# Routing pieces and shared-expert groups in another order, in a two-layer model kernel

## The chip, the cores and the metric

The kernel runs on one core of a Trainium2 chip. Its time is the device time of one execution in microseconds (us), here the median of four runs. A profile of one further execution gives each engine's instructions with their start and duration: TensorE (PE, with its weight loads as PEld), VectorE (DVE), ScalarE (ACT), GpSimd (POOL), and SyncE (SP), which issues most DMA transfers. All data are float32.

## The reference, cut to what matters

Two layers over T = 4096 tokens of D = 128 features. Each layer adds to its input an attention and a mixture of experts, both computed from the same normalised input.

```
xn = layernorm(x)
x  = x + window_attention(layernorm(xn)) + ffn0(xn)        # layer 0
xn = layernorm(x)
x  = x + gated_attention(layernorm(xn)) + ffn1(xn)         # layer 1

ffn0(xn):
    probs   = softmax(xn @ router_w + router_b)            # 8 experts
    weights = probs at the two largest, 0 elsewhere
    shared  = gelu(xn @ sw1 + sb1) @ sw2 + sb2
    experts = gelu(xn @ rw1[e] + rb1[e]) @ rw2[e] + rb2[e] # H = 256
    return shared + sum over e of weights[e] * experts[e]
```

The window attention has 16 batches of 256 tokens, 8 heads of 64, rotated queries and keys, and a softmax over 256 keys in two windows. ffn1 has 32 experts with hidden size 64, eight of them for each token.

## The kernel before, in words

The tokens lie in 8 groups of 512 (NG = 8), each four chunks of 128 (NC = 4).

**Attention of layer 0.** The order of PE, DVE, ACT and POOL is written out by hand: a loop over s from -2 to 64, in which a step s in 0 to 63 is one pair of heads and one batch, eight steps for a group g (r = s % 8). A step issues, in this order:

- `turned0(s)`: PE transposes the probabilities p (L413);
- `exponentials(s + 1)`: ACT, with a sum beside each (L395), then `evicted(s)`: ACT copies the transposed tiles to pT (L420);
- what steps before had put off: copies of the values v on ACT (L339), and in even steps the rotations of q and k (L359 to L361, on DVE and POOL);
- a piece or two of the routing, and pieces of `prepare`;
- `divided(s + 1)`: DVE's reciprocal (L401) and four products (L404);
- `scores(s + 2)`: PE (L379), then DVE's masked maximum (L384) and its negation (L388);
- `attended(s - 1)`: PE (L430), ACT (L435); and `project` of the group before at r = 2: PE (L441), ACT (L443).

The routing of a group is a generator of five pieces, `routed` with `route0` inside: (1) two normalisations, DVE with POOL's powers; (2) transposes and a copy to xnT; (3) the router's matmuls; (4) logits less their maximum on DVE, and their exponential pr_all on ACT (L220); (5) on DVE the sum of pr_all (L223), reciprocal, product, and the rank of each expert by comparisons (L196 to L205). The call of a step is

```
step(routing, 2 * g + 2 + r // 4, (1, 1, 1, 2)[r % 4])
```

so that a group's five pieces are spread over four steps, and pieces 4 and 5 come together in a step with r % 4 == 3.

`places0` (L231 to L293) turns the ranks of all tokens into row places: running counts over 32 chunks (five doublings), three matmuls that sum over partitions (pos_ps and cnt_ps, L253 the last), and from these where each token's two rows stand (slot_at), their weights (slot_w), and which expert each of 39 tiles of 256 rows has (tile_off). Before, it runs whole at s = 26. `scatter0(n)` writes chunk n's rows to x_rows in HBM, two indirect DMAs on POOL (L298) for each step from 27 to 58.

**Shared expert and expert tiles.** Behind the attention SyncE issues twelve loads of layer-1 weights (uvu to sd, L76, 1.34 MB together). `shared0(g)` transposes the weights of group g (L179; wT copied by DVE, L181), multiplies them with rb2 (L549), computes two hidden halves hs (L552, gelu at L554), adds them up with sw2 in y (L555), and adds y to yTs[g] on DVE (L556). Then 39 tiles go through four stages, each some tiles behind the other (0, 4, 5, 6): `fetched` (SyncE loads we, L572, and xt, L574, six buffers of each), `turned` (PE transposes, L585, DVE copy, L587), `hidden` (PE L594, ACT gelu L597), `down` (PE L604, DVE copy, SyncE writes y_rows, L610). Every xt waits for all scatters. The weights eg, eu and ed of layer 1, 1 MB each, are loaded last on the same queue.

**Layer 1.** `finish0(g)` gathers a token's two rows from y_rows, eight indirect DMAs on POOL for a group (L636), into yg, a single buffer; PE transposes yTs[g], DVE adds it to x (L645), adds the gathered rows with their weights (L648), and normalises; xn1T follows on PE. Routing, gated attention and 17 pairs of experts for each group stand behind it.

Of the kernel before, what the change touches and what calls it, by code (L numbers as in the profile page):

```python
# [23 lines left out]
NG = T // G  # L24
# [23 lines left out]
def two_layers(ctx: ExitStack, tc: tile.TileContext, a: dict, out: bass.AP):  # L48
# [182 lines left out]
    def places0(wk):  # L231

        nch = NG * NC
        fl = lambda t: t.rearrange("p n e -> p (n e)")
        top, sel = (wk.tile([P, nch, E0], F32, tag=f"m{i}", name=f"m{i}", bufs=1) for i in range(2))
        nc.vector.tensor_scalar(fl(sel), fl(rk_all), 2.0, None, ALU.is_lt)
        nc.vector.tensor_scalar(fl(top), fl(rk_all), 0.0, None, ALU.is_equal)
        nc.vector.tensor_tensor(fl(w0_all), fl(sel), fl(pr_all), ALU.mult)

        acc = sel  # L240
        for i in range(5):
            k = 1 << i
            nxt = wk.tile([P, nch, E0], F32, tag=f"cum{i % 2}", name=f"cum{i}", bufs=1)
            nc.vector.tensor_copy(nxt[:, :k, :], acc[:, :k, :])
            nc.vector.tensor_tensor(nxt[:, k:, :], acc[:, k:, :], acc[:, : nch - k, :], ALU.add)
            acc = nxt
        ex = wk.tile([P, nch, E0], F32, tag="ex", name="ex", bufs=1)
        nc.vector.tensor_tensor(ex, acc, sel, ALU.subtract)
        pos_ps = mm_tile("pos_ps")[:, : nch * E0]
        nc.tensor.matmul(pos_ps, upper, fl(sel), start=True, stop=False)  # L250
        nc.tensor.matmul(pos_ps, ones, fl(ex), start=False, stop=True)
        cnt = mm_tile("cnt_ps")[:, :E0]
        nc.tensor.matmul(cnt, ones, acc[:, nch - 1, :], start=True, stop=True)  # L253
        ns = T // RT
        full = wk.tile([P, E0, ns], F32, tag="full", name="full", bufs=1)
        nc.vector.tensor_tensor(
            full, cnt.unsqueeze(2).to_broadcast([P, E0, ns]), steps.unsqueeze(1).to_broadcast([P, E0, ns]), ALU.is_gt
        )
        used = wk.tile([P, E0], F32, tag="used", name="used", bufs=1)
        nc.vector.tensor_reduce(used, full, AX.X, ALU.add)  # L260
        low = wk.tile([P, E0, E0], F32, tag="low", name="low", bufs=1)
        nc.vector.tensor_tensor(
            low, used.unsqueeze(1).to_broadcast([P, E0, E0]), tie0.rearrange("p (i j) -> p i j", j=E0), ALU.mult
        )
        begin = wk.tile([P, E0], F32, tag="begin", name="begin", bufs=1)
        nc.vector.tensor_reduce(begin, low, AX.X, ALU.add)
        row0 = wk.tile([P, E0], F32, tag="row0", name="row0", bufs=1)
        nc.vector.tensor_scalar(row0, begin, float(RT), None, ALU.mult)
        pos = wk.tile([P, nch, E0], F32, tag="pos", name="pos", bufs=1)
        nc.vector.tensor_tensor(  # L270
            pos, pos_ps.rearrange("p (n e) -> p n e", e=E0), row0.unsqueeze(1).to_broadcast([P, nch, E0]), ALU.add
        )
        nc.vector.tensor_tensor(fl(sel), fl(sel), fl(top), ALU.subtract)
        for s, m in enumerate((top, sel)):
            at = wk.tile([P, nch, E0], F32, tag="at", name=f"at{s}", bufs=1)
            nc.vector.tensor_tensor(at, m, pos, ALU.mult)
            atr = wk.tile([P, nch], F32, tag="atr", name=f"atr{s}", bufs=1)
            nc.vector.tensor_reduce(atr, at, AX.X, ALU.add)
            nc.vector.tensor_copy(slot_at[:, s, :], atr)
        for s, m in enumerate((top, sel)):  # L280
            nc.vector.tensor_tensor(m, m, pr_all, ALU.mult)
            nc.vector.tensor_reduce(slot_w[:, s, :], m, AX.X, ALU.add)

        le = wk.tile([P, NT0, E0], F32, tag="le", name="le", bufs=1)
        nc.vector.tensor_tensor(
            le, begin.unsqueeze(1).to_broadcast([P, NT0, E0]), tiles.unsqueeze(2).to_broadcast([P, NT0, E0]), ALU.is_le
        )
        ex_t = wk.tile([P, NT0], F32, tag="ex_t", name="ex_t", bufs=1)
        nc.vector.tensor_reduce(ex_t, le, AX.X, ALU.add)
        nc.vector.tensor_scalar(ex_t, ex_t, -1.0, None, ALU.add)  # L290
        off = wk.tile([P, NT0], F32, tag="off", name="off", bufs=1)
        nc.vector.tensor_scalar(off, ex_t, float(P), None, ALU.mult)
        nc.vector.tensor_copy(tile_off, off)  # L293

    def scatter0(n):

# [12 lines left out]
    with first as pa:  # L309
        wk = pa.enter_context(tc.tile_pool(name="wkA", bufs=2))  # L310
# [138 lines left out]
        with tc.manual_schedule(engines={order.PE, order.DVE, order.Activation, order.Pool}):  # L449
            routing = {g: routed(g) for g in range(NG)}  # L450
            preparing = {g: prepare(g) for g in range(NG)}

            def step(gens, g, n=1):
                if 0 <= g < NG:
                    for _ in range(n):
                        next(gens[g], None)

            step(routing, 0)
            step(preparing, 0, 2)
            rotated(0)  # L460
            for f in turning:
                f()
            turning.clear()
            step(routing, 0, 2)
            step(routing, 1)
            step(preparing, 1)
            for c in range(NC):
                values(0, c)
            for f in later:
                f()  # L470
            later.clear()
            step(routing, 0, 2)
            step(routing, 1)
            rotated(1)
            for s in range(-2, NS + 1):
                g, r = divmod(s, 8)
                if 0 <= s < NS:
                    tps = turned0(s, sc.pop(s)[0])
                if 0 <= s + 1 < NS:
                    sms[s + 1] = exponentials(s + 1, *sc[s + 1])  # L480
                if 0 <= s < NS:
                    pTs[s] = evicted(s, tps)
                for f in later:
                    f()
                later.clear()
                for f in turning:
                    f()
                turning.clear()

                if s < 0:  # L490
                    step(routing, 1, 2)
                else:
                    step(routing, 2 * g + 2 + r // 4, (1, 1, 1, 2)[r % 4])
                if r == 0:
                    step(preparing, g + 1)
                if s >= 0 and r == 6:
                    step(preparing, g + 2)
                if 0 <= s + 1 < NS:
                    divided(s + 1, sc[s + 1][0], sms.pop(s + 1))
                if s + 2 < NS:  # L500
                    sc[s + 2] = scores(s + 2)
                if s >= 1:
                    attended(s - 1, pTs.pop(s - 1))

                if s % 2 and 2 <= (s + 5) // 2 < NS // 2:
                    rotated((s + 5) // 2)
                if s < 0:
                    continue
                if r == 2 and g:
                    project(g - 1)  # L510
                if r in (4, 6) and g + 1 < NG:
                    values(g + 1, r - 4)
                    values(g + 1, r - 3)
                if s == 10:
                    zero = w_a.tile([P, 2 * D], F32, tag="zero", name="zero")
                    nc.gpsimd.memset(zero, 0.0)
                    x_r0 = x_rows.rearrange("(t p c) d -> p t (c d)", p=P, c=2)
                    nc.sync.dma_start(out=x_r0, in_=zero.unsqueeze(1).to_broadcast([P, NT0, 2 * D]))
                if s == 26:
                    places0(wk)  # L520
                if 27 <= s < 59:
                    scatter0(s - 27)
            project(NG - 1)
    turn[0] = ["mm", "s", "mm", "o", "mm", "s"]

# [17 lines left out]
    with ExitStack() as pb:  # L543
# [65 lines left out]
            nc.vector.tensor_copy(y, yp)  # L609
            nc.sync.dma_start(out=yr[t], in_=y)  # L610

        for g in range(NG):
            shared0(g)
        stage = [fetched, turned, hidden, down]
        at = [0, 4, 5, 6]
        state = {}
        for t in range(NT0 + at[-1]):
            for f, d in zip(stage, at):
                i = t - d
                if 0 <= i < NT0:  # L620
                    state[i] = f(i, *state.get(i, ()))
        eg = load("eg", [P, E1 // 2, P], pool=late, eng=nc.sync)
        eu = load("eu", [P, E1 // 2, P], pool=late, eng=nc.sync)
        ed = load("ed", [P, E1 // 2, D], pool=late, eng=nc.sync)


    with ExitStack() as pc:
        wk = pc.enter_context(tc.tile_pool(name="wkC", bufs=2))
        xn1Ts, xhTs, scs = {}, {}, {}

        def finish0(g):
# [316 lines left out]
```

## Time and profile before

| | us |
|---|---|
| median of 4 runs | 1168.9 |
| lowest and highest | 1165.07, 1170.53 |
| the profiled execution's own time | 1170.06 |
| its span | 1168.0 |
| PE busy | 1005.5 (86%) |
| DVE busy | 763.9 (65%) |
| ACT busy | 441.5 (38%) |
| POOL busy | 269.9 (23%) |

The mean granted clock of TensorE is 0.933 of full speed. Times in a timeline are us from the start of the span. A timeline row is start, duration, engine, line and operation, output and inputs, and in brackets how long the engine stood idle before it and what ended that. A row of the waits is the waiting instruction, what released it, then the total in us, the count, and the longest one. The attention's last projection ends near 467, the last expert tile at 586.40, and the rest is layer 1.

### The profile page before, as it was taken

Reading aid. Unit: us, or ns where it says so; the run is one execution under the profiler, and the core shown is the slowest. Engines: PE = TensorE matmul, PEld = TensorE weight load, DVE = VectorE, ACT = ScalarE, POOL = GpSimd, SP = SyncE. Lnnn points to the kernel's source line nnn. Section 1 sums busy time; section 2 is a strip of 40 time slices with the busy share of each in tenths; the row PEclk is TensorE's granted clock in tenths of the full one; section 3 lists DMA queues with packets and bytes.
Section 4 is the critical chain, followed back from the end, with each engine's and each line's share of the span. In section 5 each row is a group of like instructions: output and inputs, shape, how many; then the busy total and the mean of one; then the engine's idle time right before and its main releaser. Section 6 shows DMA issues by size and latency. Waiting matters only on the chain.

```text
span 1168.0 us, 13430 instructions
## 1 busy us (share of the span) xinstructions
PE 1005.5 (86%) x3976; PEld 560.5 (48%) x3976; DVE 763.9 (65%) x2474; ACT 441.5 (38%) x1096; POOL 269.9 (23%) x241
## 2 busy tenths in 40 slices
PE   3686878879999999999916798998979889898998
PEld 2344455445555554369913344444435444444453
DVE  3888777788788885233335566767576675758664
ACT  1345454546576675334402222232222323223221
POOL 1111111114444441000062404124060321403010
PEclk9789888998899999999966899898989989899999
DMA  5000500000000000649813233122312313232320
GB/s 152 1 1 1 175 1 1 1 4 19 26 21 28 19 28 5 236 117 255 239 43 81 72 87 83 51 74 72 102 54 75 88 33 98 73 84 70 77 81 10
DMA packets 68472, 80.01 MB, mean 69 GB/s; under 512 B 7976, under 2 KB 43568, under 8 KB 68016
## 3 DMA queue, kind: packets, MB, share of 16 engines
q1 hardware_dynamic: 61984, 69.20, 21.2%
q0 software_dynamic: 4096, 8.40, 2.3%
q10 hardware_dynamic: 2320, 1.56, 0.5%
q8 instruction: 32, 0.52, 0.2%
q14 instruction: 40, 0.33, 0.1%
HBM read 62.09 MB, written 17.04 MB: 68 GB/s over the span
## 4 chain that ended last, share of the span: by engine, by line
PE 54%; DVE 25%; issue 7%; POOL 6%; ACT 6%; DMA 2%; POOLq 0%; ACTq 0%; DVEq 0%
PE u L821 8%; PE g L819 8%; PE z L830 7%; DVE p L404 5%; DVE p L384 5%; ACT p L395 4%; PE yr L604 3%; POOL yg L636 3%; PE h L594 3%; PE o L782 2%; PE y L441 2%; PE s L379 2%; DVE k L361 2%; PE o L430 2%; PE y L555 1%
## 5 line engine op out<-in xcount | busy, mean ns | idle before, releaser
L823 ACT ACTIVATE h<-g 128x512 f32<-128x512 f32 x128 | 76.4, 597 | 267.3 <-PE g L819 267.3
L395 ACT ACTIVATE p<-p,nm 128x256 f32<-128x256 f32 x256 | 127.1, 499 | 127.7 <-DVE nm L388 126.7
L824 DVE TENSOR_TENSOR h<-h,u 128x512 f32<-128x512 f32 x128 | 87.5, 684 | 81.7 <-PE u L821 80.4
L819 PE MATMUL g<-xn1Ts,eg 128*128 128x512 f32 x256 | 134.2, 606 | 0.0
L821 PE MATMUL u<-xn1Ts,eu 128*128 128x512 f32 x256 | 133.9, 612 | 0.0
L413 PE MATMUL t<-ident,p 128*128 128x128 f32 x512 | 78.7, 296 | 47.2 <-DVE p L404 46.3
L830 PE MATMUL z<-h,ed 128*128 128x512 f32 x224 | 117.5, 606 | 0.0
L636 POOL DMA_INDIRECT yg<-y_rows,slot_at x64 | 67.7, 1058 | 196.5 <-issue 164.8
L413 PEld LDWEIGHTS t<-ident,p 128*128 128x128 f32 x512 | 63.5, 150 | 88.0 <-issue 62.5
L379 PE MATMUL s<-k,q 64*128 64x256 f32 x512 | 96.9, 439 | 8.9 <-DVE mx L384 6.8
L361 POOL TENSOR_TENSOR q<-q,sq 128x512 f32<-128x512 f32 x32 | 40.7, 1272 | 256.5 <-DVE sq L360 256.5
L757 POOL TENSOR_TENSOR r1s<-r1s,sinr 128x512 f32<-128x512 f32 x16 | 23.2, 1453 | 325.1 <-DVE r1s L755 325.1
L384 DVE CUSTOM_DVE_ANT_0 p<-s,mask 128x256 f32<-128x256 f32 x256 | 97.5, 418 | 0.0
L826 DVE TENSOR_TENSOR h<-h,bc 128x512 f32<-128x512 f32 x128 | 90.9, 710 | 3.0
L404 DVE TENSOR_SCALAR p<-p,sm 128x256 f32<-128x256 f32 x256 | 76.7, 363 | 2.3
L821 PEld LDWEIGHTS u<-xn1Ts,eu 128*128 128x128 f32 x256 | 49.2, 197 | 56.8 <-issue 51.4
L298 POOL DMA_INDIRECT x_rows<-xn_all,slot_at x64 | 67.4, 1053 | 29.0 <-issue 16.4
L430 PE MATMUL o<-pT,v 128*64 128x256 f32 x512 | 73.4, 410 | 0.5 <-ACT oT L435 0.5
L379 PEld LDWEIGHTS s<-k,q 64*128 64x128 f32 x512 | 56.6, 204 | 34.1 <-DVE mx L384 21.4
L420 ACT COPY pT<-t 128x512 f32<-128x512 f32 x128 | 67.1, 573 | 5.5 <-PE t L413 5.5
L819 PEld LDWEIGHTS g<-xn1Ts,eg 128*128 128x128 f32 x256 | 47.9, 195 | 43.8 <-issue 37.0
L830 PEld LDWEIGHTS z<-h,ed 128*128 128x128 f32 x224 | 43.4, 196 | 52.1 <-issue 44.7
(257 smaller groups left out, 1601.5 us busy)
## 6 DMA issues: line engine op xcount, KB each, us to landing
bc<-rows_r SPq DMA_DIRECT2D x128, 256.0 KB, 4.0
we<-in_ex_dram SPq DMA_DIRECT2D x39, 257.0 KB, 3.8
x_rows<-zero SPq DMA_DIRECT2D x1, 4992.0 KB, 16.1
xt<-x_rows SPq DMA_DIRECT2D x39, 128.0 KB, 3.8
y_rows<-yt SPq DMA_DIRECT2D x39, 128.0 KB, 3.7
x<-in_x_dram SPq DMA_DIRECT2D x8, 256.0 KB, 4.7
out_dram<-out SPq DMA_DIRECT2D x8, 256.0 KB, 2.3
x_rows<-xn_all,slot_at POOLq DMA_INDIRECT x64, 2.3
```

The source lines that it names most:

```text
L379: nc.tensor.matmul(sp[h][:, i, :], q[rows, b, i * P : (i + 1) * P], k[rows, b, :], start=True, stop=True)
L384: nc.vector.tensor_tensor_reduce(out=pr[:, h, i, :], in0=sp[h][:, i, :], in1=mask[:, i, :], scale=1.0, scalar=NEG, op0=ALU.add, op1=ALU.ma ...
L395: nc.scalar.activation(row, row, AF.Exp, bias=nm[:, n : n + 1], scale=1.0, accum_out=sm[:, n : n + 1])
L404: nc.vector.tensor_scalar(row, row, sm[:, n : n + 1], None, ALU.mult)
L413: nc.tensor.transpose(tp[:, at : at + P], pr[:, h, i, j * P : (j + 1) * P], ident)
L430: nc.tensor.matmul(op[h * DH : (h + 1) * DH, :], vs[g][:, 2 * b + j, (2 * hp + h) * DH : (2 * hp + h + 1) * DH], pT[:, h, j, :], start=(j ...
L636: nc.gpsimd.indirect_dma_start(out=yg[:, 2 * c + s, :], out_offset=None, in_=y_rows, in_offset=bass.IndirectOffsetOnAxis(ap=slot_at[:, s, ...
L819: nc.tensor.matmul(gp, wg, xnT, start=True, stop=True)
L821: nc.tensor.matmul(up, wu, xnT, start=True, stop=True)
L824: nc.vector.tensor_tensor(h, h, up, ALU.mult)
L826: nc.vector.tensor_tensor(h, h, wT[n // 2][:, n % 2, :], ALU.mult)
L830: nc.tensor.matmul(zp, w, r, start=(n == 1), stop=False)
```

## The change

`places0` becomes a generator of seven pieces, one issued in each of the steps 24 to 30. The routing's five pieces go out one in each step: piece 5 of a group moves from the step with s % 4 == 3 to the next one, ahead of the following group's piece 1. The scatters run in steps 30 to 61 instead of 27 to 58. Only `shared0(0)` stays ahead of the expert tiles in the code; groups 1 to 7 stand behind them and ahead of the loads of eg, eu and ed. The pool of layer 1's tiles gets `reuse_waits="tile"`. No arithmetic is added or removed.

```diff
 def places0(wk):
         nc.vector.tensor_tensor(fl(w0_all), fl(sel), fl(pr_all), ALU.mult)
+        yield
...
             acc = nxt
+            if i == 2:
+                yield
...
         nc.tensor.matmul(cnt, ones, acc[:, nch - 1, :], start=True, stop=True)
+        yield
...
             pos, pos_ps.rearrange("p (n e) -> p n e", e=E0), row0.unsqueeze(1).to_broadcast([P, nch, E0]), ALU.add
         )
+        yield
...
             nc.vector.tensor_copy(slot_at[:, s, :], atr)
+        yield
...
             nc.vector.tensor_reduce(slot_w[:, s, :], m, AX.X, ALU.add)
+        yield
...
         nc.vector.tensor_copy(tile_off, off)
+        yield
...
-                    step(routing, 2 * g + 2 + r // 4, (1, 1, 1, 2)[r % 4])
+                    if s % 4 == 0:
+                        step(routing, s // 4 + 1)
+                    step(routing, s // 4 + 2)
+                if s == 24:
+                    placing = places0(wk)
+                if 24 <= s < 31:
+                    next(placing)
...
-                if s == 26:
-                    places0(wk)
-                if 27 <= s < 59:
-                    scatter0(s - 27)
+                if 30 <= s < 62:
+                    scatter0(s - 30)
...
-        for g in range(NG):
-            shared0(g)
+        shared0(0)
         stage = [fetched, turned, hidden, down]
...
                     state[i] = f(i, *state.get(i, ()))
+        for g in range(1, NG):
+            shared0(g)
         eg = load("eg", [P, E1 // 2, P], pool=late, eng=nc.sync)
         eu = load("eu", [P, E1 // 2, P], pool=late, eng=nc.sync)
         ed = load("ed", [P, E1 // 2, D], pool=late, eng=nc.sync)
...
-        wk = pc.enter_context(tc.tile_pool(name="wkC", bufs=2))
+        wk = pc.enter_context(tc.tile_pool(name="wkC", bufs=2, reuse_waits="tile"))
```

## The prediction

> **What bounds the kernel now.** I read the page first: engine shares, slices, then the chain that ended last.
>
> ```profile
> DVE  3888777788788885233335566767576675758664
> PE   3686878879999999999916798998979889898998
> PE 54%; DVE 25%; issue 7%; POOL 6%; ACT 6%; DMA 2%; POOLq 0%; ACTq 0%; DVEq 0%
> ```
>
> A slice is 29.2 us. Slices 2 to 16 are the attention: DVE is at 7 to 8 tenths and PE does not fill. Slices 17 to 20 (shared expert, expert tiles) are PE at 9. Slice 21 holds a hole, PE 1 and 6. So DVE sets the attention's step and PE the stage behind it. The chain says so as a sum: 54% PE, 25% DVE.
>
> Next, the waits of the attention, and the timeline of one step with s % 4 == 3.
>
> ```profile
> DVE rsm L223 <- ACT pr_all L220: 21.0, 7, 4.9
> ```
>
> ```profile
> 194.47 1.05 ACT L420 COPY pT<-t 128x512 f32<-128x512 f32 x2
> 195.41 0.24 ACT L220 ACTIVATE pr_all<-lg 128x32 f32<-128x32 f32 x1
> 195.68 0.18 DVE L223 TENSOR_REDUCE rsm<-pr_all 128x4 f32<-128x32 f32 x1 [4.79 <-ACT pr_all L220]
> 198.05 0.42 DVE L205 TENSOR_REDUCE rk_all<-gt_r 128x32 f32<-128x256 f32 x1
> 198.39 0.17 DVE L401 RECIPROCAL sm<-sm 128x4 f32<-128x4 f32 x1
> ```
>
> DVE stands 4.79 us for a routing exponential that ACT reaches only after the step's own four exponentials and two pT copies. The division (L401) needs only the step's exponentials, done by 194.5, yet starts at 198.39, behind piece 5 of the routing.
>
> Then the stretch of step 26 where places0 runs whole:
>
> ```profile
> 248.84 0.29 DVE L236 TENSOR_SCALAR m<-rk_all 128x256 f32<-128x256 f32 x1
> 254.06 0.29 DVE L256 TENSOR_TENSOR full<-cnt_ps,steps 128x128 f32<-128x128 f32 x1 [1.54 <-PE cnt_ps L253]
> 261.13 0.18 DVE L293 CAST tile_off<-off 128x39 int32<-128x39 f32 x1
> 261.23 0.17 DVE L401 RECIPROCAL sm<-sm 128x4 f32<-128x4 f32 x1
> ```
>
> It is 12.4 us of DVE in one block ahead of a division. Last, the stage behind the attention, by SyncE's timeline and by windows (columns: window, length, busy time and count of PE, PEld, DVE, ACT, POOL, granted clock, DMA share, GB/s).
>
> ```profile
> 467.18 0.34 SPq L76 DMA_DIRECT2D uvu<-in_uvu_dram  x1
> 474.18 0.43 SPq L574 DMA_DIRECT2D xt<-x_rows  x1
> 479.93 0.33 SPq L76 DMA_DIRECT2D eg<-in_eg_dram  x1
> ```
>
> ```profile
> 467.00:509.00 42.00, 41.92 (x113) 16.50 (x111) 10.17 (x16) 12.85 (x18) 0.00 (x0) 0.96 0.48 164
> 530.00:550.00 20.00, 20.00 (x145) 18.97 (x144) 7.57 (x20) 8.63 (x21) 0.00 (x0) 1.00 0.92 264
> 588.00:592.00 4.00, 0.00 (x0) 0.00 (x0) 0.00 (x0) 0.00 (x0) 1.77 (x2) 0.81 0.12 34
> 592.00:596.00 4.00, 0.00 (x0) 0.00 (x0) 1.44 (x5) 0.00 (x0) 3.09 (x4) 0.50 0.17 49
> 616.00:620.00 4.00, 4.00 (x12) 2.34 (x11) 3.20 (x23) 2.17 (x4) 0.14 (x1) 0.78 0.06 16
> ```
>
> The shared expert takes 41 us on a full PE while SyncE fetches. The tiles then run on a full PE with the DMA engines 92% busy. After them PE does nothing from 586.40 until the first layer-1 transposes at 606.44:
>
> ```profile
> 589.93 1.06 POOL L636 DMA_INDIRECT yg<-y_rows,slot_at  x1 [147.59 <-issue]
> 606.44 1.40 PE L172 MATMUL xn1T<-ident,xn 128*128 128x128 f32 x4 [19.60 <-DVE xn L151]
> ```
>
> **Routing.** Six steps with s % 4 == 3 in the steady part pay (the seventh wait is in the prologue). Exponentials done against start of L401: 68.5/72.25, 98.2/102.90, 132.1/135.82, 161.8/166.48, 194.5/198.39, 224.3/229.04. The delays sum to 25.5 us. The change puts piece 5 into the next step, ahead of its division; there pr_all was written a step ago, so the wait is gone, but the work is not: L223 to L401 is 226.34 to 229.04, 2.7 us, and DVE has no gap in those steps. 6 x 2.72 = 16.3 come back, and 25.5 - 16.3 = **-9.2 us**. Bounds: -4 if half of the wait returns as the wait of L401 for ACT p, which is late next (that wait already totals 37.5 us), and -11 if one idle microsecond of a few of those steps takes in part of piece 5.
>
> **Places.** Step 26 to 27 (from L401 to L401, 245.82 to 261.23) took 15.41 where its neighbours without places take about 5.8, and the next lost 0.3: cost now 9.9 us. Cut into seven pieces by L236 to L293, they measure 0.72, 1.55, 1.4, 1.7, 2.34, 1.57 and 1.55, 10.8 us in all; the 1.54 wait for cnt_ps falls away since its matmuls go out a step earlier. They stand in steps 24 to 30. Odd steps leave DVE about 1.26 us idle for ACT's exponentials, and the step with the projection 2.6. Pieces 2 and 6 shrink by 1.26 each, piece 4 vanishes: 10.8 - 2 x 1.26 - 1.7 = 6.6 stay. **-3.2 us**; bounds 0 (nothing hides) and -6 (all pieces find such gaps). The scatters start three steps later and still end with the attention's POOL work, since 64 of them at 2 a step occupy steps 30 to 61; the last land before the first xt is fetched. Cost nothing; if the cover went, the first tile would wait for them, 1 to 2 us.
>
> The attention, ending at A = 467.1 (last y L441), thus ends 12.4 us sooner, range 4 to 17.
>
> **The shared expert behind the tiles.** Times from A. Before: shared 41.1, tiles to 586.40 (78.2 us, 1.97 a tile of 39, with the pipeline's ends), 3.53 until the first gather: +122.8.
>
> After, step by step:
> - shared group 0: 4.8 (each of the eight takes 5.12). Then PE has nothing. SyncE's queue is as before: twelve late loads, .47 us apart, first xt issued at 474.18, A + 7.1; landing is 3.8 us by the page, so the first transposes start at **A + 11.0**. About 6 us of PE idle, which the shared groups covered before.
> - The granted clock falls: the rows above show a hole in PE with 0.81, then 0.50, and 0.78 in the first window of dense work again. At half clock for 2 to 3 us, I take +1.2 (0 to 1.7).
> - Tiles 78.2. What loses its cover here is the fetching: before, six buffers of we and xt and all three 1 MB loads eg, eu, ed were issued by 481.02, during the shared groups. Now eg stands after xt of tile 12, eu after tile 26, ed after the result of tile 30, all in SyncE's queue ahead of the next tiles' fetches. At 264 GB/s and share .92, a full DMA gives 287 GB/s: 3.1 MB take 11.0 us, and slack of .08 x 78 gives 6.3 of it back. So +4.7 if no lead is there, 0 if the six buffers carry all; the lead is 2 to 3 tiles at the start (transfers from A + 6.7, use from A + 11.0, 1.8 us of full DMA a tile), gains .08 tile with each tile, and each 1 MB load eats 2 (3.7 us). I take **+3.4** (0 to 6), and +0.3 for the thin start.
> - Shared groups 1 to 7 follow on PE. The first gather does not wait for the last of them wholly, but nearly: in the built program yg_0 lies where the wT buffers of the shared groups lay, so it waits for the rb2 matmul of group 7, six groups and 2.6 us after their start: 6 x 5.12 + 2.6 = 33.3. [...]
> - Sum: 11.0 + 1.2 + 78.5 + 3.4 + 33.3 + 0.2 = 127.6 against 122.8: **+4.8 us**, range -2 to +9.
>
> So the move does not put the shared groups beside the eight gathers (10.5 us, 1.31 apart) and the norms; only 3.4 us of PE work (two hs, four sw2 matmuls) are left beside them. The saved items are the 3.53 landing wait and these 3.4; the lost are the fetch gap, its clock and the stalls. Behind the gather the order is the same: 0.
>
> [...]
>
> **Sum.** -9.2 - 3.2 + 4.8 = -7.6. The profiled execution took 1170.06 (span 1168.0 and 2.1 around it), so 1162.5; it stands 1.2 above the median of 1168.9, so **1161.3**. I call 0.3%, 3.5 us, the bound that a measurement of this kernel can tell.
>
> **Rivals.**
> 1. The tile stage becomes bound by DMA: slower. For: 92% busy already, and xt is fetched with a lead of only about 4.8 us in tiles 13 to 16 and 27 to 30, against a landing of 3.8 at the median, 4.4 at most. Once landing under load passes 4.8 us, some 20 tiles wait; at 0.8 us each that is 16 on top of 1161.3 - 3.4: about 1174. Against: fewer transfers stand in the queue at once than in the first tiles of before. It decides when the DMA share in the tiles reaches 1.00. 7%.
> 2. The attention gains half (-5) as the freed time returns as ACT waits, and the second part costs +4 or +5: 1168.5, no change. For: L401 already waits 37.5 us for ACT. Against: in the six steps the exponentials were done 4 us before. 14%.
> 3. The gather does not wait for rb2 of group 7, so the shared groups fill the hole of 19.6 us: second part -10 instead of +4.8, 1147. Against: the memory places above. 6%.
> 4. My forecast: 73%, its own range 1154 to 1166.
>
> Together, 1152 to 1169 leaves out most of cases 1 and 3 and little else. Faster by over 0.3%: case 4 nearly whole, case 3 and a little of 2: .75; within: .16; slower: .09.
>
> **What would show it.** Right: L223's wait under 5 us in all; no step over 9 us between divisions near 24 to 31; the last y L441 near 455; PE idle some 6 us before the first xtT; the tile stage 80 to 84 us; the first gather 127 to 128 us behind the attention's end. Wrong: L401's wait for ACT p up by over 5 us; DMA share at 1.00 with PE under 19 of 20 us in the tiles; a gather that starts before the shared groups.

## The result: the change costs 0.2%

The changed kernel takes 1173.06 us in the median of 52 runs (1163.69 to 1177.94), the kernel before 1168.73 in 78. The ratio is 1.0022, 95% interval 1.0011 to 1.0032: slower, where 1161.3 was forecast. The means, 1170.8 and 1168.3, lie 2.5 us apart and the medians 4.3. Neither shows what matters. The 52 times fall into two groups with nothing between 1168.6 and 1171.5: 20 of them lie at 1163.7 to 1168.6, and 32 at 1171.5 to 1177.9. The profile taken with the result is of the lower group (1164.33, span 1162.5), 1.8 us above the forecast for the profiled execution (1162.5). That this is near is luck in part, as the last sections show. A second profile of the same kernel (r1_after_again, below) is of the upper group: 1177.32, span 1175.6.

The page of the changed kernel (lower group), the same lines as before:

```profile
DVE  3888787978878884333235556767576676758664
PE   4677777888999997899936797998979889899998
PE 53%; DVE 24%; issue 8%; POOL 6%; ACT 4%; DMA 4%; SPq 1%; POOLq 0%; ACTq 0%; DVEq 0%
```

Nothing here warns of a loss: the attention is as DVE-bound as it was, and ends a little sooner. The waits (instruction, releaser, total, count, longest) show the routing's wait gone, as intended, and two others longer, the first of each pair below from before the change:

```profile
PE t L413 <- DVE p L404: 46.3, 22, 6.4
PE t L421 <- DVE p L412: 54.8, 17, 7.5
DVE sm L401 <- ACT p L395: 37.5, 26, 3.2
DVE sm L409 <- ACT p L403: 48.5, 31, 3.8
DVE rsm L223 <- ACT pr_all L220: 0.3, 1, 0.3
```

L223 waited 21.0 us before. PE's wait for the divided rows is 8.5 us longer, and the division's wait for ACT 11.0. The timeline of one step with s % 4 == 0 shows where the first comes from:

```profile
162.26 0.17 DVE L223 TENSOR_REDUCE rsm<-pr_all 128x4 f32<-128x32 f32 x1
168.94 0.17 DVE L409 RECIPROCAL sm<-sm 128x4 f32<-128x4 f32 x1
169.64 1.94 PE L421 MATMUL t<-ident,p 128*128 128x128 f32 x8 [7.46 <-DVE p L412]
```

Piece 5 now stands ahead of the next group's piece 1 and of the division. DVE is 6.7 us at the routing (1.13 of it a wait for POOL), and PE has nothing for 7.46 us. The eight transposes behind the hole take 1.94 us, against 1.04 elsewhere: the granted clock is 0.50 there.

The places, in the same timeline:

```profile
238.32 0.42 DVE L251 TENSOR_TENSOR ex<-cum,m 128x256 f32<-128x256 f32 x1
238.80 0.70 PE L254 MATMUL pos_ps<-ex,ones 128*128 128x256 f32 x2 [2.73 <-DVE ex L251]
239.55 1.14 PE L387 MATMUL s<-k,q 64*128 64x256 f32 x8
248.05 0.18 DVE L409 RECIPROCAL sm<-sm 128x4 f32<-128x4 f32 x1 [3.78 <-ACT p L403]
```

The matmul of ex stands in PE's queue ahead of the scores, and waits 2.73 us for the third piece, the last work of DVE in that step ahead of the division. The scores, the attended rows and the 3.7 us projection all follow late, then ACT's exponentials, and the next division waits 3.78 us.

The stage behind the attention, by SyncE, PE and POOL, and by windows (columns as before):

```profile
457.46 0.34 SPq L76 DMA_DIRECT2D uvu<-in_uvu_dram  x1
482.19 0.49 SPq L76 DMA_DIRECT2D eg<-in_eg_dram  x1
```

```profile
467.23 0.69 PE L597 MATMUL xtT<-ident,xt 128*128 128x128 f32 x2 [5.08 <-DMA xt<-x_rows]
583.46 1.06 POOL L649 DMA_INDIRECT yg<-y_rows,slot_at  x1 [143.16 <-PE y L561]
600.15 1.45 PE L172 MATMUL xn1T<-ident,xn 128*128 128x128 f32 x4 [13.62 <-DVE xn L151]
```

```profile
467.00:480.00 13.00, 12.26 (x67) 10.55 (x68) 3.71 (x10) 4.19 (x10) 0.00 (x0) 0.78 0.88 257
500.00:520.00 20.00, 20.00 (x145) 18.97 (x144) 7.56 (x20) 8.64 (x22) 0.00 (x0) 1.00 1.02 321
```

PE is empty for 5.08 us ahead of the first tile (`xtT`, its transposes), and in the first 13 us of the tiles the granted clock is 0.78 in the mean. DMA carries 321 GB/s in the middle, and PE does not wait there. The gather waits for L561 of group 7, as foreseen.

Three marks make the rest readable: A, when SyncE issues its first late load (the attention's end); the first gather; the first xn1T.

| profiled execution | span | A | first gather | xn1T |
|---|---|---|---|---|
| before | 1168.0 | 467.2 | A + 122.8 | A + 139.3 |
| changed, lower group | 1162.5 | 457.5 | A + 126.0 | A + 142.7 |
| changed, upper group | 1175.6 | 468.9 | A + 127.1 | A + 143.8 |

Of the 13.1 us between the two profiles of one kernel, 11.5 lie in the attention. There the whole gain of 9.7 us is lost again. And 1.8 of these 9.7 lie ahead of the first division, where the change moves nothing; a run with the same attention (r2, below) has 0.2 there.

### The profile page after: what moved, and what is told of

It reads as the page before. It is cut to its first block, busy times and chain, and to the rows that moved or that the text cites. A ratio compares the mean times of both kernels' runs of the same rounds, so it can differ in the third digit from the quotient of the medians.

```text
span 1162.5 us, 13395 instructions
## 1 busy us (share of the span) xinstructions
PE 993.1 (85%) x3976; PEld 556.7 (48%) x3976; DVE 764.5 (66%) x2474; ACT 441.3 (38%) x1096; POOL 269.5 (23%) x241
## 4 chain that ended last, share of the span: by engine, by line
PE 53%; DVE 24%; issue 8%; POOL 6%; ACT 4%; DMA 4%; SPq 1%; POOLq 0%; ACTq 0%; DVEq 0%
PE u L834 8%; PE g L832 8%; PE z L843 7%; DVE p L412 5%; DVE p L392 4%; ACT p L403 4%; POOL yg L649 3%; PE y L449 3%; PE o L795 2%; PE h L606 2%; PE yr L616 2%; PE s L387 2%; PE o L438 2%; DMA we<-in_ex_dram 2%; DVE k L369 2%
## 5 line engine op out<-in xcount | busy, mean ns | idle before, releaser
L387 PE MATMUL s<-k,q 64*128 64x256 f32 x512 | 91.4, 436 | 8.4 <-DVE mx L392 6.6
L387 PEld LDWEIGHTS s<-k,q 64*128 64x128 f32 x512 | 54.1, 202 | 30.3 <-DVE mx L392 18.2
```

Of the source, the lines that this page charges most:

```text
L387: nc.tensor.matmul(sp[h][:, i, :], q[rows, b, i * P : (i + 1) * P], k[rows, b, :], start=True, stop=True)
```

## The experiments

**The same kernel again**, for a profile of the upper group.

> The changed kernel once more, for a second profile and its spread. Its times fall into two groups, 1164 to 1168 and 1172 to 1178 us, and the profile at hand is of the lower one. If the upper group comes from the tile stage (a fetch too late, or a slower clock there), a profile of that group shows the first gather some 9 us later behind the attention's end than the 126.0 us here. If it comes from layer 1, the gather stands at 126 and the rest is 9 us longer. If from the attention, the last y L449 is near 466 instead of 457.

It came out as the third case, the attention: 12 runs, five at 1164.9 to 1165.8 and seven at 1175.9 to 1177.8, and a profile of the upper ones. A step is counted here from one division to the next. The divisions run beside those of the lower profile within 0.6 us up to step 17. Then single steps are longer: 18, 19, 22, 27 and 30 by 0.5 to 1.6 us, and further on those that have the rotations and the projection (50 with 51, 58 with 59: 8.4 + 6.7 us against 6.2 + 5.7) and the short steps at the end, which have neither (60: 6.9 against 4.4). The lower profile has one such pair of its own, 42 with 43. Step 26 is shorter, by 1.0. The windows around step 58 tell why:

```profile
424.00:426.00 2.00, 0.52 (x5) 0.34 (x4) 1.94 (x6) 0.37 (x1) 1.53 (x3) 1.00 0.00 0
426.00:428.00 2.00, 1.68 (x11) 0.96 (x10) 1.93 (x12) 0.80 (x3) 1.70 (x2) 0.93 0.19 66
428.00:430.00 2.00, 2.00 (x8) 1.17 (x10) 0.80 (x4) 2.00 (x8) 1.18 (x2) 0.50 0.10 33
430.00:432.00 2.00, 2.00 (x9) 0.86 (x10) 1.97 (x11) 0.36 (x2) 0.00 (x0) 0.50 0.11 37
432.00:434.00 2.00, 2.00 (x3) 0.97 (x4) 0.53 (x4) 2.00 (x8) 0.00 (x0) 0.50 0.00 0
434.00:436.00 2.00, 2.00 (x12) 1.03 (x11) 1.43 (x3) 0.59 (x3) 0.00 (x0) 0.86 0.00 0
```

PE is thin for two microseconds (0.52 of 2.00 busy), and then runs at half clock from 427.7 to 434.6 (worked out from the clocks of the rows at its two ends, 0.93 and 0.86). In the three rows of 0.50 PE is full, and DVE waits in two of them (0.80 and 0.53 of 2.00, ACT being full there too): 1.16 us for ACT's exponentials and 1.44 for a product of PE. The attention has ten stretches at half clock in the lower profile and 14 in the upper (mean granted clock from 240 to 455: 0.98 and 0.93); 428 to 435 and 452 to 458 are among those that the lower one lacks. The kernel before has one too, at its step 34:

```profile
294.00:300.00 6.00, 6.00 (x17) 2.85 (x18) 3.29 (x17) 4.34 (x17) 1.00 (x2) 0.50 0.07 23
```

**Each part alone.** Routing and places without the shared part:

```diff
-        shared0(0)                      # of the changed kernel
+        for g in range(NG):
+            shared0(g)
...
-        for g in range(1, NG):
-            shared0(g)
```

> Routing and places in pieces as in the change, the shared expert as before it. My theory: the attention ends 9.7 us sooner, as in the changed kernel's profile, and all behind it is as before: 9 to 10 us faster than before, about 1159. If the attention is what has two lengths, this kernel has two groups of times too; if the stage behind is, it has the spread of before (1163 to 1172, shifted).

Ratio 0.9961 (0.9939 to 0.9984), 1162.58; eight times at 1159.6 to 1162.9, four at 1169.6 to 1170.6: two groups without the shared part. The shared part alone:

> The shared expert's groups 1 to 7 behind the tiles, routing and places as before. My theory: gather 3 us later behind the attention's end in the lower group, 12 in the upper: two groups, about 1171 and 1180, median 10 or more slower than before. If the two groups come from the attention, one group near 1172.

Ratio 1.0047 (1.0029 to 1.0065), 1173.62, six times at 1171.7 to 1176.5 with no gap over 2.1 us; first gather at A + 126.5. The lower of my two figures held, the upper group near 1180 did not come. Six times are few, but r2 has two groups without this part. Then routing alone, with places0 whole at step 26:

> Only the routing in one piece a step; places whole at step 26, shared expert as before. My theory: 8.5 us saved up to step 24, and the places as before: lower group near 1160, with or without an upper group. If the pieces of the places are what brings the upper group, this kernel has one group; if the 7.5 us holes of PE in the steps with s % 4 == 0 are, it has two.

Ratio 0.9930 (0.9910 to 0.9951), 1158.89, and no time above 1163.7. Last, the pieces of the places alone:

> Only the places in seven pieces (and the scatters three steps later); routing and shared expert as before. From the profiles so far (steps 24 to 31 of the changed kernel, less piece 5, against those of before) my theory now: 1 to 2 us slower than before in its lower group, since the wait of the scores of step 26 for ex eats what the odd steps hide; the prediction's theory: 3.2 us faster. If the pieces of the places are what brings the upper group of times, some of these times stand 9 to 10 us above the others; if the routing's 7.5 us holes are, none does.

Ratio 1.0067 (1.0044 to 1.0090), 1177.86. This is worse than either theory: of seven times, three stand at 1169.9 to 1174.2 and four at 1177.9 to 1179.5. In its profile (1174.22) steps 24 to 31 take 58.2 us against 55.3 before, and the steps behind them 4.5 us more than before, with the long steps 58 to 60 of the upper profile. So this part, which was to gain, loses, and an upper group comes with it. The profile is of the lower three, though, so it does not show what the upper four have more. The three parts alone give -0.70, +0.67 and +0.47%, in sum +0.44, beside the +0.22 of the whole; the intervals of the parts allow for that difference.

**Keeping PE busy.** If thin stretches of PE make the groups, useless matmuls in them must take the groups away. They write columns of the bank of o that nobody reads:

```diff
...
-            nc.scalar.copy(oTs[g][:, hp, b * N : (b + 1) * N], op)
+            nc.scalar.copy(oTs[g][:, hp, b * N : (b + 1) * N], op[:, :N])
+            if (s + 1) % 2 == 0:
+                for _ in range(24 if (s + 1) % 4 == 0 and s < 24 else 3):
+                    nc.tensor.matmul(op[:, N:], ident, cosq, start=True, stop=True)
```

> The changed kernel with extra matmuls of no use on TensorE in the attention, into unread columns of the bank of o: 24 (128x256) behind the attended step of s = 0, 4 to 24, where PE stood 7.5 us for DVE, and 3 in every other even step. My theory, that the upper group of times is half-clock stretches of TensorE in the attention (428 to 435 and 452 to 458 in the slow profile): with PE kept busy the granted clock stays at 1.00 from step 0 on, the upper group is gone, and the times gather in one group at 1155 to 1165. The rival, that the groups come from DMA or from the order of scatters: the two groups stay, both some us longer by the work added.

The groups went, five times at 1201.7 to 1204.0, but I had sized the filler wrongly: each matmul shows as two instructions, 24 of them took 10.6 us in a hole of 7.5, and all that stands behind them in PE's queue came late. The edit puts 24 in six steps, 4, 8 and so on to 24, and none in step 0, which has no `attended`. So again with 13, and one in the other even steps but those with the projection:

> The changed kernel with fewer useless matmuls: 13 behind the attended step of s = 0, 4 to 24 (some 5.8 us by the 0.22 us each that the earlier run showed, in a hole of 7.5), one in the other even steps but those with the projection. My theory, that half-clock stretches make the upper group and cost the lower one a few us too: one group of times, at 1158 to 1166, median some 9 us under the changed kernel's. The rival, that the matmuls cost as much as the clock gives back: the groups gone, but the median not under 1168.

Twelve times in one group, 1160.2 to 1165.0; 1163.07, ratio 0.9951 (0.9938 to 0.9965). Work of no use added to PE made the changed kernel 10 us faster in the median. From 240 to 455, the windows of the lower profile, of the upper one and of this kernel:

```profile
240.00:455.00 215.00, 199.50 (x1049) 109.26 (x1046) 172.00 (x655) 135.19 (x425) 87.20 (x80) 0.98 0.06 21
```

```profile
240.00:455.00 215.00, 199.17 (x994) 108.50 (x996) 169.00 (x636) 128.72 (x405) 87.31 (x80) 0.93 0.06 21
```

```profile
240.00:455.00 215.00, 199.35 (x1076) 112.23 (x1073) 171.73 (x654) 135.41 (x425) 87.37 (x80) 1.00 0.06 21
```

PE's busy time is the same 199 us in all three; the clock is 0.98, 0.93 and 1.00, and PE did 1049, 994 and 1076 instructions, of which the filler is 28 in the last. That the upper group is half-clock stretches of the attention is shown by this run.

**The matmuls of the places behind the scores of step 26** (the third piece ends ahead of them, and they are issued behind `attended`):

> The changed kernel with the three matmuls of the places moved behind scores and attended of step 26 in PE's queue. My theory, that the places in pieces saved nothing because PE stood 2.7 us for ex (L251) ahead of the scores of step 26: steps 26 and 27 shorten together from 18.7 to 14 or 15 us, attention 4 us sooner, in either group. The rival, that DVE's own work is what these steps cost: no change of theirs over 1 us.

```profile
239.39 0.70 PE L255 MATMUL pos_ps<-ex,ones 128*128 128x256 f32 x2 [0.46 <-DVE ex L251]
246.47 0.18 DVE L410 RECIPROCAL sm<-sm 128x4 f32<-128x4 f32 x1 [2.39 <-ACT p L404]
```

Steps 26 and 27 take 8.2 + 7.2 = 15.4 us instead of 18.7 (19.3 in the upper profile), and the lower times move down by 3: nine at 1160.6 to 1166.2. Three stand at 1174.2 to 1174.4, no lower than the middle of the 32 (1173.9). The profile is of these, with A = 465.6 against 468.9 in the upper profile, and a mean granted clock of 0.923 in both: the stretches at half clock stay. Median 1163.54, ratio 0.9969 (0.9945 to 0.9993).

**yg at another place:**

```diff
         xn1Ts, xhTs, scs = {}, {}, {}
+        wk.tile([P, NC, 256], F32, tag="v1", name="place_v")
+        wk.tile([P, 2, G], F32, tag="u", name="place_u", bufs=1)
```

> The changed kernel with yg at another place (two unused tiles ahead of it in the pool), so that the gathers wait for y_rows alone. My theory: the first gather stands 3.5 us behind the last expert tile (96 us behind the attention's end instead of 126), all eight run beside the shared groups, and xn1T follows the last shared group by some 8 us, at 137 instead of 142.7: 5 to 6 us faster than the changed kernel in the same group. The rival, that the gathers are not what the norms wait for: no change.

```profile
554.69 1.06 POOL L651 DMA_INDIRECT yg<-y_rows,slot_at  x1 [113.87 <-PE y L567]
596.47 1.45 PE L172 MATMUL xn1T<-ident,xn 128*128 128x128 f32 x4 [8.39 <-DVE xn L151]
```

With A = 458.3 the first gather is at A + 96.4 and xn1T at A + 138.2, against 142.7. The middles of both groups are about 3.5 us lower (six times at 1158.3 to 1165.2, six at 1169.2 to 1171.3). So the wait for L561 was real, and its price was 4.5 us in the profile, not the 30 us by which the gather moved: PE is busy with the shared groups to A + 130 in this run.

**Which half of the places brings the upper group?** In p3 the scatters also run three steps later. That half alone, on the kernel before:

> The kernel before, with the scatters in steps 30 to 61 instead of 27 to 58, nothing else. If the later scatters (POOL and DMA work in steps 59 to 61, whose steps were the thinnest) bring the stretches at steps 58 to 60: an upper group some 6 to 10 us above the times of before. If the pieces of the places bring them: the times of before, within 1 us.

Twelve times at 1163.5 to 1167.1, ratio 0.9978 (0.9965 to 0.9990): no upper group, a little faster. So the pieces bring it, by themselves or together with the later scatters; no run has the pieces without them. And routing alone once more:

> Routing only, once more. My theory: it has the two near groups that its six times showed (1158 and 1163.5) and none at 1168 or above. If the holes of its steps with s % 4 == 0 bring the upper group, a third of the times stand at 1168 to 1170.

1157.2 to 1163.4, ratio 0.9923 (0.9902 to 0.9943). Twelve times in all, nine at 1157.2 to 1159.5 and three at 1163.4 to 1163.6: two groups again, but 4 us apart, and none 10 us up.

**What the findings point to.** Piece 5 in the odd step, where DVE has room (`if s % 4 == 1` for `if s % 4 == 0`, places whole):

> Routing only, as in p1_routing_only, but piece 5 (L223 to L205) one step later, at s % 4 == 1, where DVE stands 1.26 us for ACT's exponentials. My theory: the step at s % 4 == 0 goes back from 12.88 to 10.16 us, the next one grows from 4.38 by 1.4: 1.3 us in each of six steps, 7 to 8 us less than p1_routing_only (1158.9), about 1151. The rival, that the odd step has no room left since PE or ACT set it: no gain over 2 us.

1149.38, ratio 0.9839 (0.9815 to 0.9862): steps of 10.18 and 5.74 us instead of 12.88 and 4.38, 1.34 less a pair, as expected. Its profile still has two stretches at half clock late in the attention, with steps 50 and 58 at 8.5 us each, though the places are whole. The second part mended, on routing alone: two shared groups ahead of the tiles, yg at its own place, and eg, eu, ed tied behind the last tile's weights:

```diff
-        shared0(0)
+        for g in range(2):
+            shared0(g)
...
+            tc.add_manual_dep(ins.ins, lastw[-1].ins.name, ...)     # eg, eu, ed
```

> Routing only, and the shared expert with two groups ahead of the tiles instead of one, eg, eu and ed behind the last tile's weights instead of among the tiles, and yg at a place of its own. My theory of the second part, that it loses by the 5 us hole ahead of the first tile, by the three loads among the tiles and by the gathers that wait for group 7: first tile 10.2 us behind the attention's end without a hole, tiles 78 to 79 us instead of 82.4, xn1T near 129 instead of 137.7 behind the attention's end, so 8 to 9 us under p1_routing_only: about 1150. The rival, that the end of the norms is set by DVE whatever stands before: no change against p1_routing_only.

1152.15, ratio 0.9865 (0.9842 to 0.9888). Its profile has the first xtT at A + 10.3 without a hole, tiles in 79.1 us and xn1T at A + 129.7: the 8 us that were expected, in the profile; in the medians 6.7 of them.

> The two together: piece 5 at s % 4 == 1, and the second part of b1. If both theories hold and do not meet, about 1143.

1141.56, ratio 0.9784 (0.9759 to 0.9808). With a filler on top, lighter still (8 in each large hole, one in the other even steps):

> b2_both with the useless matmuls, 8 behind the attended step of s = 0, 4 to 24, and one in the other even steps but those with the projection. b2 had one stretch at half clock in the steady steps (step 58, 3 us). My theory: gone, 1138 to 1140 in one group. The rival, that the matmuls' own time takes it back: 1142 or more.

1139.32 (1134.5 to 1139.9), ratio 0.9738 (0.9716 to 0.9761): 30 us under the kernel before, the fastest here. Its interval overlaps that of b2, so the filler's share is not settled.

## Why the prediction was wrong, step by step

- **Routing, -9.2: right.** Up to step 24 the lower profile gained 8.5 us; alone the part gives 0.7 to 0.8%, 8.2 and 9.0 us. L223's wait is 0.3 us. What I did not say is that the moved work stretches PE's hole to 7.5 us; p2 shows that half of the moved work would have had room one step later.
- **Places, -3.2: the step that failed, in sign.** Alone they cost 0.67%, 7.8 us. Their own steps are the smaller share of that: 2.9 us in the profile of p3, and 1.4 between the lower profile and that of routing alone (59.4 and 58.0 us for steps 24 to 31). The steps behind, 4.5 us in the profile of p3, are the next point, the clock. The odd steps hid their pieces as I had counted (step 25 grew by 0.1, step 29 not at all). The error is the sentence "the 1.54 wait for cnt_ps falls away since its matmuls go out a step earlier". The wait moved to PE's queue, where it holds back scores, attended rows and projection: steps 26 and 27 took 18.7 us where I had counted about 13.4 (6.2 + 5.8 and 1.4 of piece 3). In step 26 DVE also stood 1.6 us for two products that PE made at half clock (223.6 to 233.8). Piece 4, which I took as hidden by the projection, stands in the step that this makes late. Taking the matmuls from the front of the queue gave 3.3 us of it back.
- **The clock in the attention: a term that was missing.** I weighed the granted clock only at the new hole ahead of the tiles. The profile before had rows of 0.5 in the attention too: its step 34 takes 8.39 us where steps 32 and 36 take 6.2, in a stretch at half clock from 294 to 300. I took the attention's length as one number, and it is one of several: 457.5 and 468.9 for the same program. The range of the forecast held the lower group, 20 of 52 runs, and none of the upper.
- **The shared part, +4.8: right in sum, with luck in its terms.** Alone +0.47%, 5.5 us (3.4 to 7.6). Of its terms: first tile A + 9.8 (11.0 predicted), tiles 82.4 us (83.1 with clock and stalls), then to the gather 33.9 (33.5), in sum +3.3 in the lower profile and +4.3 in the upper. But the tiles' 4.2 us over before are not what I had counted. The first 5.5 us of them run at half clock (0.50 from 465.9 to 472.8, with the first transposes at 467.2), an estimated 2.8 us lost; no run shows the 1.2 us that the sum has for this, nor its bound of 1.7. And PE stands 1.9 us in the whole stage against 0.5 before, of it 0.71 and 0.65 for weights (3.4 and 0.3 counted). The clock was priced too low and the loads too high. No run shows the 0.2 us that the sum has between the rb2 matmul and the gather; in both profiles of the changed kernel the gather starts 0.8 us behind that matmul's end.
- **The rivals.** That DMA bounds the tiles: the share reached 1.02 from 500 to 520 and PE was still busy for 20.00 of 20 us, so no. (Its landing of xt, "4.4 at most", I had misread: one took 4.9 us before.) That the gather does not wait: excluded in this kernel, and worth 3.5 to 4.5 us where it was made true, not 15. The rival of no change had the wait for ACT right (48.5 us for 37.5), but named the routing as what loses it.

The near hit in the lower group was luck in part: the attention gained 9.7 us there and not 12.4, with the 1.8 ahead of the first division among them, and the shared part cost less than counted.

What stays open: why the pieces, more than the routing's longer holes, put so many runs on the pattern with stretches at steps 58 and 60. No run here tells which piece does it. The stretch at step 58 is not theirs alone, since p2 (step 58 at 8.5 us) and b2 (3 us of it) have it with the places whole; the one at step 60 stands in r1 (0.50 from 452 to 458), and m1 (7.0 us) and p3 have the long step there; all three have the pieces and the later scatters. The profile of p3 is of its lower three times, so these stretches are not all that sets its groups apart.

## What to carry to other kernels

When work is cut into pieces to fill one engine's gaps, follow what each piece feeds: a small matmul that waits for the last vector instruction of a step belongs behind the work that could have gone first, since PE took the matmuls in the order of issue (the scores stood 2.73 us behind the one of ex, and no longer once it was issued behind them). A wait that is removed by moving work is only gone if the step that takes the work had room; for the routing's piece 5 the odd step had room for half, the full one for none. And where one kernel's times fall into groups, take a profile of each before explaining a median.

## What the runs showed that I had not expected

Half clock did not need a long idle of PE. In the stretch above, the longest gap before it that the trace shows is 1.4 us (PE 0.52 busy in 2 us), and 6.8 us at half clock followed. With the holes of 7.46 us (0.50 from 165.6 to 172.4) and of 5.08 us ahead of the first tile (465.9 to 472.8) it lasted no longer, 6.8 us each, of which 2.8 and 5.5 stand behind the end of the hole. In the attention the chip gave one program two lengths 11.5 us apart, and useless matmuls, 0.22 us for each of their instructions, took that away.
